# The first slice of x loaded with batch and step on the partitions and turned by TensorE, and Wx's pieces re-dealt over two DMA queues

## The chip, the cores and the metric

The kernel runs on one core of a Trainium2 chip. A core has TensorE (PE in the profile; PEld is its weight load), VectorE (DVE), ScalarE (ACT), GpSimd (POOL) and SyncE (SP); SP, ACT and POOL issue DMAs here. The metric is the device time of one execution in microseconds (us): 312.71 us is the median of three runs of the kernel before (312.63 to 312.9).

## The reference

An LSTM runs over x, and its hidden states go through a three-layer network whose weights are +1 or -1; the result is added to x.

```python
# x: (32, 64, 256)   cond: (32, 256) = first h   Wx, Wh: (256, 1024)   b: (1024,)
xW = einsum('ntd,dg->ntg', x, Wx) + b
for t in range(64):
    a = xW[:, t] + h @ Wh
    i, f, o = sigmoid(a[:, :256]), sigmoid(a[:, 256:512]), sigmoid(a[:, 512:768])
    g = tanh(a[:, 768:])
    c = f * c + i * g
    h = o * tanh(c)
    hs[:, t] = h
y = concat([hs, -hs], -1)
y = relu(s0 * y @ sign(k0)) * 2      # k0: (512, 1024) of bool
y = relu(s1 * y @ sign(k1)) * 2      # k1: (1024, 1024)
out = x + s2 * y @ sign(k2)          # k2: (1024, 256)
```

All is float32.

## The kernel before, in words

**The recurrence.** Batch N = 32, T = 64 steps, D = H = 256. The 128 partitions of the gate tiles are four column quarters q of 64 columns times 32 batch rows, so every product for a gate is four matmuls side by side, one for each quarter, with 32 output partitions each (`x_part`, L242; `gates_from_h`, L301). An x product takes as stationary operand xT, the turned x of one step (128 rows of D by 32 batch rows), and streams the columns of Wx. D is 256, so there are two parts k = 0 and 1; part k holds the rows 2p + k on partition p. A PSUM bank (`x_bank`) holds two steps. The gates lie in four slots, slot 0 the candidate g, slots 1, 2 and 3 the gates i, f, o. A float32 product is two passes on TensorE, so one product appears as two MATMUL records.

**The first eight steps.** The kernel cannot start the recurrence before the x products of the first steps exist. Before the loop TensorE does, in the order of the text (it is written out by hand, each engine executes its own part of it in that order): ten matmuls on a tile of zeros, two into the gate banks (L641) and eight more as a warm-up (L643); then the products for k = 0, slots 1 and 2, for all eight steps; k = 0, slots 0 and 3, for all eight; the bias, which is spread over the partitions by sixteen passes with a row of ones (`copy_bias`, L654) and copied by VectorE; and k = 1, all slots, step by step, where each finished bank is evicted with the bias added (`evict_x`, L258). Then come steps 8 to 11, and the loop over t, which mixes `gates_from_h` of each step with further x products (until step 21) and with the feed-forward network of finished blocks.

**The first loads.** `load_x(0, 0, ...)` fetches x of steps 0 to 7 in four DMAs of 64 KB, quarter by quarter, so that a row of 64 columns (256 bytes) is the unit; the tile has (quarter, batch) on the partitions. VectorE turns it by 32x32 blocks (`turn_x`, L226; the two calls are L644 and L645). Wx comes in six DMAs: SP carries slots 1 and 2 of k = 0, then of k = 1 (256 KB each); ACT carries slots 0 and 3 of k = 0, then of k = 1 (128 KB each). Then both queues carry x of steps 8 to 15, then Wh. GpSimd's queue carries the first h, three pieces of the bias and the three scales. A DMA gets one of eight completion semaphores in turn, so a ninth waits on its queue for the first to land, and what stands behind it on that queue waits too.

**Buffers.** x tiles rotate over four buffers, working tiles ("act") over 24, PSUM has two banks for the gates, four of the tag "pf" (x products and the warm-up's target) and two of the tag "po" (`ps_o`; the bias first).

Of the kernel before, what the change touches and what calls it, by code (L numbers as in the profile page):

```python
# [29 lines left out]
F32 = mybir.dt.float32  # L33
# [3 lines left out]
ALU = mybir.AluOpType  # L37
# [4 lines left out]
def lstm_ffn(ctx: ExitStack, tc: tile.TileContext, x, cond, wx_d, wh_d, b_d, k0_d, k1_d, k2_d, s0_d, s1_d, s2_d, out):  # L42
    nc = tc.nc
    P = 128
    N, T, D = x.shape
    H = cond.shape[1]
    G = 4 * H
    NQ = 4
    HQ = H // NQ
# [3 lines left out]
    SB = 16  # L53
    NB = T // SB
    TB = SB * N
    SH = 4
# [5 lines left out]

    FIRST_CHORE = 2
    W2_STEP = 24
    WARM_UP = 8

    SUM_STEP = 28

    const = ctx.enter_context(tc.tile_pool(name="const", bufs=1))
    wpool = ctx.enter_context(tc.tile_pool(name="wx", bufs=1))  # L70
    xpool = ctx.enter_context(tc.tile_pool(name="x", bufs=4))
# [7 lines left out]
    ps_o = ctx.enter_context(tc.tile_pool(name="ps_o", bufs=2, space=PSUM))  # L79
    ctx.enter_context(tc.manual_schedule())  # L80

    def act(shape, dtype, name):
        return apool.tile(shape, dtype, tag="act", name=name)


    xq = {}

    def load_x(i, half, engines, part=slice(0, SB // 2)):
        if part.start == 0:
            xq[i, half] = xpool.tile([P, SB // 2, HQ], F32, tag="x", name=f"x{i}_{half}")  # L90
        t0 = i * SB + half * (SB // 2)
        for q in range(NQ):
            engines[q % len(engines)].dma_start(
                out=xq[i, half][q * N : (q + 1) * N, part],
                in_=x[:, t0 + part.start : t0 + part.stop, ts(q, HQ)],
            )
# [5 lines left out]
    wx = wpool.tile([P, 2, G], F32, tag="wx", name="wx")  # L102
# [2 lines left out]
    w2 = const.tile([P, 2, FC1, P], F32R, name="w2")  # L105

    warm = const.tile([P, 40], F32, name="warm")
    nc.vector.memset(warm, 0.0)
    idle = const.tile([P, 512], mybir.dt.bfloat16, name="idle")
    nc.vector.memset(idle, 0.0)  # L110

    first = warm[:, 4 : 4 + N]
    nc.vector.memset(first[:1], 1.0)
# [4 lines left out]
    def load_gates(t, w_d, slots, engines, chunks=slice(0, 2)):  # L118

        w_rows = w_d.rearrange("(p b) g -> p b g", b=2)  # L120
        s0, n, g0 = slots[0], len(slots), GATES[slots[0]]
        if len(engines) == 1:
            halves = [slice(0, P)]
        else:
            halves = [slice(0, P // 2), slice(P // 2, P)]
        for engine, half in zip(engines, halves):
            engine.dma_start(
                out=t[half, chunks, s0 * H : (s0 + n) * H], in_=w_rows[half, chunks, g0 * H : (g0 + n) * H]
            )


    both = [nc.sync, nc.scalar]
    load_x(0, 0, both)
    for k in range(2):
        load_gates(wx, wx_d, (1, 2), [nc.sync], slice(k, k + 1))
        for slot in (0, 3):
            load_gates(wx, wx_d, (slot,), [nc.scalar], slice(k, k + 1))
    load_x(0, 1, both)
    load_gates(wh, wh_d, (1, 2), both)
    load_gates(wh, wh_d, (0,), [nc.scalar])  # L140
    load_gates(wh, wh_d, (3,), [nc.sync])

    nc.scalar.activation(warm[:, 1:2], warm[:, :1], AF.Sigmoid)
    h_first = const.tile([P, HQ], F32, name="h_first")
    nc.gpsimd.dma_start(out=h_first, in_=cond.rearrange("n (q j) -> q n j", q=NQ))
    b_rows = b_d.rearrange("(o g h) -> o g h", o=1, g=4)
    nc.gpsimd.dma_start(out=b_row[0][:1, :1], in_=b_rows[:, 3:])
    nc.gpsimd.dma_start(out=b_row[0][:1, 1:], in_=b_rows[:, :1])
    nc.gpsimd.dma_start(out=b_row[1][:1], in_=b_rows[:, 1:3])
    scales = []  # L150
    for i, s_d in enumerate((s0_d, s1_d, s2_d)):
        s = const.tile([P, 1], F32, name=f"s{i}")
# [7 lines left out]
    for i in range(2):  # L160
        t = act([P, 2, F0], U8, f"k0_{i}")
# [62 lines left out]
    xT = {}  # L224

    def turn_x(i, half, part=slice(0, SB // 2)):  # L226
        if part.start == 0:
            xT[i, half] = act([P, SB // 2, 2, N], F32, f"xT{i}_{half}")
        nc.vector.transpose(
            xT[i, half][:, part], xq[i, half][:, part].rearrange("p t (j b) -> p t b j", b=2)  # L230
        )
# [10 lines left out]
    def x_part(p, t, k, slots, start):  # L242

        i, s = divmod(t, SB // 2)
        for q in range(NQ):
            nc.tensor.matmul(  # L246
                p[q * N : (q + 1) * N, t % 2, slots],
                xT[i // 2, i % 2][:, s, k, :],
                wx_q[:, k, q, slots],
                start=start,  # L250
                stop=False,
                skip_group_check=True,
            )

    def x_bank(t):
        return ps_f.tile([P, 2, 4, HQ], F32, tag="pf", name=f"px{t}")

    def evict_x(p, t):  # L258
        xg[t] = gpool.tile([P, 2, 4 * HQ], F32, tag="xg", name=f"xg{t}")
        b = bias.rearrange("p g j -> p (g j)").unsqueeze(1).to_broadcast([P, 2, 4 * HQ])  # L260
        load[0] += 1
        nc.vector.tensor_tensor(xg[t], p.rearrange("p t g j -> p t (g j)"), b, ALU.add)  # L262
# [374 lines left out]
    outputs = deque()  # L637

    p_idle = ps_f.tile([P, TB], F32, tag="pf", name="p_idle")
    for g in gate_banks:  # L640
        nc.tensor.matmul(g, idle[:, :P], idle, start=True, stop=True)  # L641
    for n in range(WARM_UP):
        nc.tensor.matmul(p_idle, idle[:, :P], idle, start=True, stop=True)  # L643
    turn_x(0, 0, slice(0, SB // 4))  # L644
    turn_x(0, 0, slice(SB // 4, SB // 2))  # L645
    for i in range(4):
        load_bits(i)
    for half in range(2):
# [5 lines left out]
    def copy_bias():  # L654
        p_bias = ps_o.tile([P, 4, HQ], F32, tag="po", name="p_bias")
        for q in range(NQ):
            for i, t in enumerate(b_row):
                nc.tensor.matmul(  # L658
                    p_bias[q * N : (q + 1) * N, 2 * i : 2 * i + 2],
                    first,  # L660
                    t.rearrange("p g (q j) -> p q g j", q=NQ)[:, q],
                    start=(i == 0),
                    stop=True,
                    skip_group_check=True,
                )
        nc.vector.tensor_copy(bias, p_bias)

    banks = [x_bank(t) for t in range(0, SB // 2, 2)]
    for slots in (slice(1, 3), slice(0, 4, 3)):
        for t in range(SB // 2):  # L670
            x_part(banks[t // 2], t, 0, slots, t % 2 == 0 and slots.start == 1)
    copy_bias()
    for t in range(SB // 2):
        x_part(banks[t // 2], t, 1, slice(0, 4), False)
        if t % 2:
            evict_x(banks[t // 2], t - 1)
            if t == 1:
                turn_x(0, 1)
# [89 lines left out]
```

## Time and profile before

| | |
|---|---|
| median of three runs | 312.71 us (312.63 to 312.9) |
| the profiled execution's own time | 312.31 us |
| its span, first to last instruction | 310.5 us |
| outside the span | 1.8 us |
| TensorE busy | 304.5 us, 98% of the span |
| VectorE, ScalarE, GpSimd busy | 178.1, 142.0, 6.6 us |
| DMA | 10.89 MB, mean 35 GB/s; in the first 1/40 of the span 192 GB/s |

A row of a timeline gives start, duration, engine, line, operation and tiles; several like instructions in a row are merged with a count. The chain of work is followed back from the last instruction to what released it, so its pieces add up to the span. For a DMA the profile gives the time of its issue and the time from there to its landing.

### The profile page before, as it was taken

The numbers are of one execution on the slowest core, as the hardware profiler recorded it, in microseconds if no ns is written. First come the engines' busy times: TensorE is split into PE (matmuls) and PEld (weight loads), VectorE is DVE, ScalarE is ACT, GpSimd is POOL, SyncE is SP. The second block draws the span as 40 slices with busy tenths as digits, with TensorE's granted clock in tenths as the row PEclk, the third lists the DMA queues.
The fourth block names the chain that finished last, engine by engine and source line by source line (L and its number), as shares of the span: only waits on it lengthen the run. The fifth ranks groups of instructions, "written<-read, shape, count | busy, mean of one in ns | idle before, by whom it ended". The sixth has DMA issues, their size and how long they took to land.

```text
span 310.5 us, 9798 instructions
## 1 busy us (share of the span) xinstructions
PE 304.5 (98%) x4138; PEld 242.7 (78%) x4138; DVE 178.1 (57%) x530; ACT 142.0 (46%) x512; POOL 6.6 (2%) x24
## 2 busy tenths in 40 slices
PE   8999999999999999999999999999999999999994
PEld 4888888788777777777777777777777777899993
DVE  2566767777673444355754445567554434698543
ACT  0225566774564543435633434355443333886220
POOL 5300000000000000000000000000000000000000
PEclk9999999999999999999999999999999999999999
DMA  6874001142000000000010000000310000131002
GB/s 192 206 196 99 5 19 38 36 95 65 3 2 0 2 2 0 3 2 0 2 38 22 14 3 0 2 2 13 92 34 2 3 0 2 31 79 27 2 0 69
DMA packets 30587, 10.89 MB, mean 35 GB/s; under 512 B 27720, under 2 KB 29768, under 8 KB 30544
## 3 DMA queue, kind: packets, MB, share of 16 engines
q1 hardware_dynamic: 27136, 8.66, 11.2%
q10 hardware_dynamic: 3168, 1.57, 2.0%
q8 instruction: 32, 0.52, 0.7%
q0 software_dynamic: 240, 0.04, 0.1%
q14 instruction: 11, 0.09, 0.1%
HBM read 8.16 MB, written 2.10 MB: 33 GB/s over the span
## 4 chain that ended last, share of the span: by engine, by line
PE 97%; DVE 1%; ACT 0%; issue 0%; ACTq 0%
PE p L617 30%; PE gates L305 20%; PE px L246 18%; PE p L591 8%; PE po L604 7%; PE gates L452 4%; PE po L561 2%; PE r L452 2%; PE x L452 2%; PE p L479 2%; PE p_idle L643 1%; PE gates L641 0%; DVE a_7l L362 0%; DVE o L388 0%; PE p_bias L658 0%
## 5 line engine op out<-in xcount | busy, mean ns | idle before, releaser
L305 PEld LDWEIGHTS gates<-wh,hist 128*32 128x32 f32 x2016 | 54.6, 109 | 22.3 <-issue 13.4
L305 PE MATMUL gates<-wh,hist 128*32 128x192 f32 x2016 | 68.1, 275 | 0.0
L246 PE MATMUL px<-wx,xT 128*32 128x256 f32 (+1 forms) x1168 | 60.5, 353 | 0.1
L322 ACT ACTIVATE sig<-gates 128x128 f32<-128x128 f32 x64 | 17.7, 277 | 80.6 <-PE gates L305 80.4
L246 PEld LDWEIGHTS px<-wx,xT 128*32 128x32 f32 x1168 | 42.4, 110 | 11.3 <-DVE c_first L652 0.7
L326 DVE TENSOR_TENSOR kept<-sig,c 128x64 f32<-128x64 f32 x63 | 14.2, 225 | 50.0 <-ACT sig L322 49.7
L332 ACT ACTIVATE th<-c 128x64 f32<-128x64 f32 x64 | 16.4, 257 | 31.4 <-DVE c L330 31.4
L334 DVE TENSOR_TENSOR h<-sig,th 128x64 f32<-128x64 f32 x64 | 14.4, 225 | 20.7 <-ACT th L332 20.7
L262 DVE TENSOR_TENSOR xg<-px,bias 128x512 f32<-128x512 f32 x32 | 21.2, 671 | 2.8 <-PE px L246 2.3
L316 ACT COPY gates<-xg 128x192 f32<-128x192 f32 x64 | 20.0, 313 | 1.3 <-DVE xg L262 1.3
L591 PE MATMUL p<-hhi,w 128*128 128x512 f32 x48 | 19.3, 402 | 0.0
L591 PE MATMUL p<-hlo,w 128*128 128x512 f32 x48 | 19.1, 398 | 0.0
L339 DVE STREAM_TRANSPOSE hist<-h 128x64 f32<-128x64 f32 x64 | 15.7, 245 | 2.4
L330 DVE TENSOR_TENSOR c<-kept,new 128x64 f32<-128x64 f32 x64 | 14.4, 224 | 2.2
L324 ACT ACTIVATE sig<-gates 128x64 f32<-128x64 f32 x64 | 14.9, 233 | 0.1
L323 ACT ACTIVATE cand<-gates 128x64 f32<-128x64 f32 x64 | 14.0, 218 | 0.0
L328 DVE TENSOR_TENSOR new<-sig,cand 128x64 f32<-128x64 f32 x64 | 13.9, 217 | 0.0
L317 ACT COPY gates<-xg 128x64 f32<-128x64 f32 x64 | 13.0, 203 | 0.0
L591 PEld LDWEIGHTS p<-hhi,w 128*128 128x128 f32 x48 | 9.0, 188 | 2.2
L591 PEld LDWEIGHTS p<-hlo,w 128*128 128x128 f32 x48 | 9.0, 188 | 2.0
L211 ACT ACTIVATE w<-bits,nsgn,sgn 128x1024 fp32r<-128x1024 uint8 x8 | 9.9, 1241 | 0.0
L617 PE MATMUL p<-a_7h,w 128*128 128x512 f32 x24 | 9.9, 413 | 0.0
(249 smaller groups left out, 602.8 us busy)
## 6 DMA issues: line engine op xcount, KB each, us to landing
x<-in_x_dram SPq DMA_DIRECT2D x60, 64.0 KB, 2.8
out_dram<-o SPq DMA_DIRECT2D x28, 64.0 KB, 1.8
bits<-in_L_ffn_k_dram SPq DMA_DIRECT2D x10, 128.0 KB, 3.2
wx<-in_L_cond_Wx_dram SPq DMA_DIRECT2D x2, 256.0 KB, 4.2
wx<-in_L_cond_Wx_dram ACTq DMA_DIRECT2D x4, 128.0 KB, 4.6
wh<-in_L_cond_Wh_dram ACTq DMA_DIRECT2D x2, 256.0 KB, 5.6
wh<-in_L_cond_Wh_dram SPq DMA_DIRECT2D x2, 256.0 KB, 6.2
k<-in_L_ffn_k_dram SPq DMA_DIRECT2D x2, 256.0 KB, 3.1
```

The lines of the kernel that those rows point to most:

```text
L246: nc.tensor.matmul(p[q * N : (q + 1) * N, t % 2, slots], xT[i // 2, i % 2][:, s, k, :], wx_q[:, k, q, slots], start=start, stop=False, ski ...
L262: nc.vector.tensor_tensor(xg[t], p.rearrange("p t g j -> p t (g j)"), b, ALU.add)
L305: nc.tensor.matmul(g[q * N : (q + 1) * N], hT[:, k, :], wh_q[:, k, q, slots], start=False, stop=(k == 1), skip_group_check=True,)
L316: nc.scalar.copy(gates[0], x_t[:, :3])
L322: nc.scalar.activation(sig[:, 0:2, :], gates[0][:, 1:3], AF.Sigmoid)
L324: nc.scalar.activation(sig[:, 2, :], gates[1][:, 0], AF.Sigmoid)
L332: nc.scalar.activation(th, c, AF.Tanh)
L339: nc.vector.transpose(hT, h.rearrange("p (j b) -> p b j", b=2))
L452: nc.tensor.matmul(bank[pair][:, i], a(k)[:, ts(2 * pair + i, P)], b(k, n), start=first and i == 0 and k == 0 and n == 0, stop=last and k ...
L591: nc.tensor.matmul(p, w0[:, k, ts(m, P)], a[:, k, :], start=(n == 0), stop=(n == 3))
L604: nc.tensor.matmul(po[m], w2[:, m, k], a1[k][n], start=(k == 0 and n == 0), stop=(k == FC1 - 1 and n == 1))
L617: nc.tensor.matmul(p1[m], w1[:, k, ts(m, P)], a0[k][n], start=(k == 0 and n == 0), stop=(k == FC0 - 1 and n == 1),)
```

## The change

The first eight steps of x are loaded as `x_first`: (batch, step) on the partitions, batch outermost, four steps at a time, so that a row of all 256 columns (1 KB) is the unit. Steps 0 to 3 come in two DMAs of 64 KB, one on each queue, steps 4 to 7 in one of 128 KB on ACT. TensorE turns each half by two transposes against an identity (`turn_first`), and VectorE copies the two results from PSUM into the same xT tile as before, with step and batch in the order that the products want. GpSimd makes the identity (`ident`: a memset and an affine select) ahead of its DMAs.

Wx comes in six DMAs again: k = 0 slots 1 and 2 by halves of the partitions on both queues; slot 3 on SP and slot 0 on ACT, each k = 0; then k = 1, slots 1, 2 and 3 in one DMA of 384 KB on SP and slot 0 on ACT. On GpSimd's queue the bias goes ahead of the first h.

The warm-up is three matmuls before the first turn and two behind it in place of eight; the zeros tile is 128 columns, read four times over, in place of 512, and is set first. The products of k = 0 are done by halves of four steps: slots 1 and 2, then slots 0 and 3, with the second turn between the two of the first half. The bias comes behind the first two steps of k = 1 in place of ahead of them.

```diff
-    WARM_UP = 8
+    WARM_UP = (3, 2)
...
+    idle = const.tile([P, P], mybir.dt.bfloat16, name="idle")
+    nc.vector.memset(idle, 0.0)
     nc.vector.memset(warm, 0.0)
-    idle = const.tile([P, 512], mybir.dt.bfloat16, name="idle")
-    nc.vector.memset(idle, 0.0)
...
+    ident = act([P, P], F32, "ident")
+    nc.gpsimd.memset(ident, 1.0)
+    nc.gpsimd.affine_select(
+        out=ident, in_=ident, pattern=[[-1, P]], compare_op=ALU.is_equal, fill=0.0, base=0, channel_multiplier=1
+    )
...
     both = [nc.sync, nc.scalar]
-    load_x(0, 0, both)
-    for k in range(2):
-        load_gates(wx, wx_d, (1, 2), [nc.sync], slice(k, k + 1))
-        for slot in (0, 3):
-            load_gates(wx, wx_d, (slot,), [nc.scalar], slice(k, k + 1))
+    x_first = xpool.tile([P, 2, D], F32, tag="x", name="x_first")
+    for s, engine in enumerate(both):
+        engine.dma_start(out=x_first[ts(s, P // 2), 0], in_=x_in[ts(s, N // 2), :SH])
+    load_gates(wx, wx_d, (1, 2), both, slice(0, 1))
+    nc.scalar.dma_start(out=x_first[:, 1], in_=x_in[:, SH : 2 * SH])
+    load_gates(wx, wx_d, (3,), [nc.sync], slice(0, 1))
+    load_gates(wx, wx_d, (0,), [nc.scalar], slice(0, 1))
+    load_gates(wx, wx_d, (1, 2, 3), [nc.sync], slice(1, 2))
+    load_gates(wx, wx_d, (0,), [nc.scalar], slice(1, 2))
     load_x(0, 1, both)
...
-    h_first = const.tile([P, HQ], F32, name="h_first")
-    nc.gpsimd.dma_start(out=h_first, in_=cond.rearrange("n (q j) -> q n j", q=NQ))
     b_rows = b_d.rearrange("(o g h) -> o g h", o=1, g=4)
     nc.gpsimd.dma_start(out=b_row[0][:1, :1], in_=b_rows[:, 3:])
     nc.gpsimd.dma_start(out=b_row[0][:1, 1:], in_=b_rows[:, :1])
     nc.gpsimd.dma_start(out=b_row[1][:1], in_=b_rows[:, 1:3])
+    h_first = const.tile([P, HQ], F32, name="h_first")
+    nc.gpsimd.dma_start(out=h_first, in_=cond.rearrange("n (q j) -> q n j", q=NQ))
...
     p_idle = ps_f.tile([P, TB], F32, tag="pf", name="p_idle")
+    zeros = idle.unsqueeze(1).to_broadcast([P, TB // P, P])
+
+    def warm_up(n):
+        for _ in range(n):
+            nc.tensor.matmul(p_idle, idle, zeros, start=True, stop=True)
+
+    def turn_first(i):
+        p = ps_o.tile([P, 2, N, SH], F32, tag="po", name=f"px_first{i}")
+        for k in range(2):
+            nc.tensor.transpose(p[:, k].rearrange("p n t -> p (n t)"), x_first[:, i, k::2], ident)
+        for k in range(2):
+            nc.vector.tensor_copy(xT[0, 0][:, ts(i, SH), k, :], p[:, k].rearrange("p n t -> p t n"))
+
+    xT[0, 0] = act([P, SB // 2, 2, N], F32, "xT0_0")
     for g in gate_banks:
-        nc.tensor.matmul(g, idle[:, :P], idle, start=True, stop=True)
-    for n in range(WARM_UP):
-        nc.tensor.matmul(p_idle, idle[:, :P], idle, start=True, stop=True)
-    turn_x(0, 0, slice(0, SB // 4))
-    turn_x(0, 0, slice(SB // 4, SB // 2))
+        nc.tensor.matmul(g, idle, zeros, start=True, stop=True)
+    warm_up(WARM_UP[0])
+    turn_first(0)
+    warm_up(WARM_UP[1])
...
     banks = [x_bank(t) for t in range(0, SB // 2, 2)]
-    for slots in (slice(1, 3), slice(0, 4, 3)):
-        for t in range(SB // 2):
-            x_part(banks[t // 2], t, 0, slots, t % 2 == 0 and slots.start == 1)
-    copy_bias()
+    for i in range(2):
+        for slots in (slice(1, 3), slice(0, 4, 3)):
+            for t in range(i * SH, (i + 1) * SH):
+                x_part(banks[t // 2], t, 0, slots, t % 2 == 0 and slots.start == 1)
+            if i == 0 and slots.start == 1:
+                turn_first(1)
     for t in range(SB // 2):
         x_part(banks[t // 2], t, 1, slice(0, 4), False)
+        if t == 1:
+            copy_bias()
         if t % 2:
             evict_x(banks[t // 2], t - 1)
```

## The prediction

> **What bounds the kernel now.** The page first: TensorE is the chain from end to end.
>
> ```profile
> span 310.5 us, 9798 instructions
> PE 304.5 (98%) x4138; PEld 242.7 (78%) x4138; DVE 178.1 (57%) x530; ACT 142.0 (46%) x512; POOL 6.6 (2%) x24
> PE 97%; DVE 1%; ACT 0%; issue 0%; ACTq 0%
> ```
>
> TensorE runs its text in order, so a microsecond saved ahead of the loop is saved at the end, if nothing behind it has to wait for a load instead. The change touches only the head, so next comes the chain of the first 20 us (start, duration, what).
>
> ```profile
> 0.91 0.28 DVE idle L110
> ...
> 1.24 1.03 PE gates L641 x2
> 2.27 3.23 PE p_idle L643 x8
> 5.51 1.89 PE px L246 x64
> 7.39 0.12 issue
> 7.51 1.96 PE px L246 x64
> 9.47 0.47 PE p_bias L658 x16
> 9.94 6.91 PE px L246 x128
> 16.84 0.83 PE gates L305 x28
> ```
>
> The first product can't be used before 5.5; ten idle matmuls fill the time. One hole is left, at 7.39: between the two halves of part k = 0, where slots 0 and 3 are wanted. The timeline and the DMA answers for the issues in short windows say what was waited for (last column of the latter: us from issue to landing).
>
> ```profile
> 1.66 0.92 SPq L127 DMA_DIRECT2D wx<-in_L_cond_Wx_dram  x2
> 1.69 2.29 ACTq L127 DMA_DIRECT2D wx<-in_L_cond_Wx_dram  x4
> 4.32 0.77 DVE L229 STREAM_TRANSPOSE xT<-x 128x256 f32<-128x256 f32 x2 [2.02 <-DMA x<-in_x_dram]
> ...
> x<-in_x_dram ACTq DMA_DIRECT2D x1, 64.0 KB, 2.4
> x<-in_x_dram SPq DMA_DIRECT2D x1, 64.0 KB, 2.2
> ...
> wx<-in_L_cond_Wx_dram SPq DMA_DIRECT2D x1, 256.0 KB, 3.4
> wx<-in_L_cond_Wx_dram SPq DMA_DIRECT2D x1, 256.0 KB, 5.0
> wx<-in_L_cond_Wx_dram ACTq DMA_DIRECT2D x2, 128.0 KB, 5.2
> wx<-in_L_cond_Wx_dram ACTq DMA_DIRECT2D x1, 128.0 KB, 4.6
> ```
>
> x is there at 4.1 and turned at 5.1. Wx slots 1 and 2 of k = 0 land at 1.66 + 3.4 = 5.0, of k = 1 at 2.15 + 5.0 = 7.1. ACT's second piece, slot 3 of k = 0, issued at 2.19, lands at 7.4: it ends the hole. ACT's last, issued at 3.54, lands at 8.1. So this stretch has two limits: TensorE's work, and 1.25 MB (x's 256 KB, Wx's 1 MB) that take until 8.1 to land.
>
> **The change part by part.**
>
> *Earlier warm-up.* The zeros are set first and are a quarter as wide: 0.1 us (the 40-column row of L108, 0.09) in place of 0.09 + 0.27. TensorE starts at about 1.0, 0.25 earlier. Five idle matmuls at the pace of the row (3.23 / 8 = 0.40; starts 0.43 apart) end at 3.1.
>
> *x_first.* The first two pieces are 64 KB each, first in their queues, like the two whose rows show 2.2 and 2.4 from 0.73: landed at 2.9 to 3.1, when the five matmuls end. Rows of 1 KB in place of 256 bytes may help; I take nothing for it.
>
> *Identity.* GpSimd's first own instruction stands at 1.25. The memset costs between 0.1 (L756, one column) and 0.49 (VectorE, 512 columns). The affine select isn't in the trace: between 0.19 (GpSimd's one-column rows) and 0.7 (VectorE, 512 columns). Ready at 1.5 to 2.4, hidden behind x, unless GpSimd must set itself up first: it ran no arithmetic before 8.38.
>
> ```profile
> 1.25 0.88 POOL L145 DMA_DIRECT2D h_first<-in_cond_dram  x1 [0.81 <-POOLq L756]
> ...
> 3.60 1.69 POOL L153 DMA_DIRECT2D s<-in_L_ffn_s_dram  x3
> ...
> 8.38 0.24 POOL L169 TENSOR_SCALAR sgn<-s 128x1 f32<-128x1 f32 x1 [3.10 <-DMA s<-in_L_ffn_s_dram]
> ```
>
> Its last DMA issue ends at 5.29, and the 3.1 us up to 8.38 are put down to the scale's landing, so a set-up of anything up to 3.1 would be hidden there. I take zero, since the row names the DMA as the last to come, and keep 3.1 for a rival.
>
> The Trainium skill, "GPSIMD Engine Reference", section 2.1 Instruction dispatch, speaks against this part: the first call of a freshly loaded GpSimd kernel also pays about 6 us of code loading that no instruction shows. The 3.1 us above leave no room for that, if this is the same case; with 6 us the identity would come at 7.9, the products start at 9.4, and the time would be an estimated 317. No run here shows which instructions need such a load.
>
> *The transposes.* Two per turn, two passes each as for every float32 product here. A pass costs no less than 0.03 (p_bias: 0.47 / 16) and no more than an exposed 128-column weight load and a product pass in a row, 0.19 + 0.11. So a turn is 0.12 to 1.2. I take 0.7 for the first, because the idle matmuls of 512 columns start 0.43 apart there and those of L617 later 0.2 to 0.25: TensorE is at half its pace; and 0.4 for the second. First turn: 3.1 to 3.8.
>
> *Copies, and the first product.* A VectorE copy from PSUM cost 0.42 for 256 columns (L666); for 128 I take 0.3 (bounds 0.21 and 0.42). The first copy releases part k = 0 at 3.8 + 0.06 + 0.3 + 0.1 = 4.3; the copy for k = 1 is wanted much later. Two idle matmuls hold TensorE until 3.8 + 0.85 = 4.65. Slots 1 and 2 have 128 KB less ahead of them than before: at the 299 GB/s of the window from 3.1 to 3.9 (shown below) 0.45 earlier, 4.55, and no later than 5.0. So the first product stands at 4.65, against the chain's 5.51: 0.85 gained.
>
> *Then the wait that takes the hole's place.* TensorE does slots 1 and 2 of four steps (half of 1.89: 0.95), then the second turn (0.4): 6.0. Next it wants slots 0 and 3 of k = 0. Before, 1.89 us of other work was done by the time slot 3 landed, now half of it. Behind that landing stand 0.98 + 0.95 + 0.98 = 2.9 us up to the end of k = 0, which before was at 9.47. So the break-even is a landing of slot 0 at 9.47 - 2.9 = 6.55.
>
> Slot 0 is fourth on ACT's queue: 64 + 128 + 128 KB ahead of it and its own 128 make 448 KB. If SP's queue moves as many, 896 KB have moved. The ladder of landings before: 512 KB at 5.0, 1280 KB at 8.1; between them 896 KB fall on 6.55. If SP's 384 KB go whole ahead of slot 0, it is 1152 KB, 7.6; if ACT is a turn ahead, 768 KB, 6.0. I take 6.6: the middle, and a little for the 1 KB rows. End of k = 0: 9.5. Nothing gained, nothing lost.
>
> *Behind it, at zero.* k = 1 has all landed by about 8. The bias matmuls are the same sixteen; their rows of b are issued some 0.7 to 1.2 later (identity ahead, first h behind) and took 4.5 to 4.7: landed by 9, wanted past 10. The first h slips by about 2 us to 7.5; it is turned at 14.04. The scales slip by 1 us and are wanted in the loop. VectorE loses two turns (0.77) and gets four copies; it waits for TensorE there (4.8 us before L666). SP and ACT issue nine DMAs in place of ten, and x of steps 8 to 15 and Wh stand behind them as before; TensorE wants Wh at 16.8, and its last piece landed at about 14.9 (issued at 8.1, some 6.2 to 6.8 us), so 1.9 us cover it. If that cover went, the first step would wait for it.
>
> **The sum.** 0.85 earlier start, less 0.4 for the second turn, less 0.6 of wait (6.0 to 6.6), plus the old hole of 0.1: zero, or 0.1 lost, 312.4 against the profiled execution's 312.31. That execution lies 0.4 under the median of 312.71, so I say 312.8.
>
> **The rivals.**
>
> *Slot 0 lands in time* (6.0 or earlier). For it: loads that start with fewer, longer rows, and GpSimd's DMAs later. Against it, the windows of the head: with x's short rows gone the DMA still fell to half for a while (last column GB/s).
>
> ```profile
> 3.10:3.90 0.80, 0.80 (x4) 0.28 (x2) 0.00 (x0) 0.00 (x0) 0.80 (x3) 1.00 1.05 299
> 3.90:4.70 0.80, 0.80 (x4) 0.25 (x3) 0.38 (x2) 0.00 (x0) 0.80 (x2) 1.00 0.71 149
> ```
>
>  Then TensorE sets the end: 6.0 + 2.9 = 8.9, 0.55 gained, 312.15; with a landing by 5.6, a start at 4.4 and a turn of 0.25, 0.95 gained, 311.75.
>
> *Slot 0 lands last* (7.2 to 7.6), because an engine serves SP's 384 KB whole before it turns to ACT's queue. For it: SP was served first before (its slots of k = 0 at 5.0, ACT's slot 3 at 7.4). It gives 7.4 + 2.9 = 10.3, 0.8 lost, 313.5; it decides from 7.2 on.
>
> *The identity is late.* Each 0.1 by which it passes 3.1 moves the turn and the two idle matmuls behind it; it decides from 3.7 on, where the wait for slot 0 is used up (3.7 + 0.7 + 0.85 + 0.95 + 0.4 = 6.6). With the full 3.1 us and the long memset and select (5.5): turn to 6.2, idle matmuls to 7.05, then 0.95 + 0.4 + 2.9 = 11.3: 1.8 lost, 314.5. At 4.0, 313.0.
>
> *TensorE stays at half pace* into the products, because it idles or transposes where eight unbroken matmuls stood. Before, the pace had doubled by 5.5: 64 products of 128 columns took 1.89, as 128 of 256 columns took 6.91. What ends by 6.6 is free behind the wait. If it lasts through the first half of k = 0, that ends at 4.65 + 1.9 + 0.7 + 1.95 = 9.2, and k = 0 at 11.1: 1.65 lost, 314.35.
>
> On this the Trainium skill, "TensorE: Matmul & The Clock Gate", Part 4: PE-mode transpose, says that transposes don't count as busy for the clock as matmuls do. By it alone the 0.7 us of the first turn would delay full pace by about as much, most of which the wait hides; no row here shows a transpose.
>
> **How the numbers follow.** Forecast (slot 0 at 6.1 to 7.1: 312.3 to 313.3) 0.42; in time 0.24; last 0.19; late identity 0.09; half pace 0.06. The bound of 0.2%, about what a measurement of this kernel can tell from no change, is 312.09 and 313.34. Faster: most of the in-time case, 0.22. Slower: the last three but for their mild ends, and the upper edge of the forecast, 0.36. Within: 0.42. The range leaves out the best of the in-time case and the worst of the late ones: 311.8 to 314.1; the forecast's own is 312.3 to 313.3.
>
> **What would show it.** Right: the first transpose of `turn_first` near 3.1; the first x product near 4.6; the second turn near 5.6; then a hole of TensorE that ends with a landing of Wx between 6.1 and 7.1; the end of k = 0 near 9.5; no hole behind it. Wrong: an identity after 3.7, products 0.06 us apiece in place of 0.03, a wait for Wh near 16, or no hole at all.

## The result: 0.6% slower, and the profile after

The changed kernel takes 314.76 us in the median of six runs (313.63 to 315.22), the kernel before 312.84 us beside it: a ratio of 1.0063, 95% interval 1.0053 to 1.0073. That is 1.9 us lost where 0.1 was forecast. The profiled execution took 315.07 us, span 313.3 us. The changed kernel, measured once more later, took 314.08 us (313.68 to 315.87) against 312.63: 1.0058 (1.0037 to 1.0079).

The page still shows one bound, TensorE, and 2.4 us more of its busy time; the DMA now appears in the chain.

```profile
span 313.3 us, 9803 instructions
PE 306.9 (98%) x4139; PEld 242.0 (77%) x4139; DVE 178.1 (57%) x532; ACT 142.0 (45%) x512; POOL 7.1 (2%) x26
PE 96%; DMA 1%; DVE 1%; SPq 0%; issue 0%; ACT 0%; ACTq 0%
```

The chain of the first 20 us of the changed kernel (start, duration, what) answers to the one shown of before:

```profile
0.78 0.68 SPq L145
...
1.52 3.79 DMA wx<-in_L_cond_Wx_dram
5.31 0.14 issue
5.45 1.94 PE px L260 x32
7.38 0.63 PE px_first L663 x2
8.01 4.22 PE px L260 x112
12.23 0.48 PE p_bias L685 x16
12.71 6.11 PE px L260 x109
```

Two things are to be seen. The first product stands at 5.45, not at 4.65: it waits for a half of Wx's slots 1 and 2. And from there the first 32 products take 1.94 us, where 64 took 1.89 before. The bias now has 16 records of k = 1 ahead of it (16 x 0.054 = 0.86), so 12.23 here compares with 9.47 + 0.86 = 10.33 before: the end of k = 0 is 1.9 late. That is nearly all of the loss; in the profiled execution two short stalls of TensorE, about 0.25 each at 15.1 and 25.8, which no wait explains, add to it: the first step's h comes 2.2 late, the end of the span 2.8.

TensorE's timeline for the same stretch shows the pace in the durations.

```profile
1.86 1.49 PE L658 MATMUL p_idle<-idle 128*128 128x512 bf16 x3
3.56 0.67 PE L663 MATMUL px_first<-ident,x_first 128*128 128x128 f32 x2 [0.21 <-DMA x_first<-in_x_dram]
4.03 1.06 PE L658 MATMUL p_idle<-idle 128*128 128x512 bf16 x2
5.45 1.94 PE L260 MATMUL px<-wx,xT 128*32 128x128 f32 x32 [0.36 <-DMA wx<-in_L_cond_Wx_dram]
7.31 0.70 PE L663 MATMUL px_first<-ident,x_first 128*128 128x128 f32 x2
7.94 4.29 PE L260 MATMUL px<-wx,xT 128*32 128x128 f32 x112
```

The second turn takes 0.70, as long as the first; where the pace was full it took about 0.50 in the runs below. The trace's record of the granted clock begins with the rise to full pace: at 5.20 us of the span before, at 9.22 us after. (That record holds nothing ahead of the first rise, and a view of the clock prints 1.00 there; the pace of that stretch is read from durations.)

The issues and landings, from the timeline of the queues and from the DMA answers for short windows (last column of these: us from issue to landing):

```profile
0.79 0.65 ACTq L145 DMA_DIRECT2D x_first<-in_x_dram  x1
1.47 0.60 ACTq L130 DMA_DIRECT2D wx<-in_L_cond_Wx_dram  x1
1.52 1.96 SPq L130 DMA_DIRECT2D wx<-in_L_cond_Wx_dram  x3
2.75 1.09 ACTq L130 DMA_DIRECT2D wx<-in_L_cond_Wx_dram  x2
```

```profile
x_first<-in_x_dram SPq DMA_DIRECT2D x1, 64.0 KB, 2.6
wx<-in_L_cond_Wx_dram ACTq DMA_DIRECT2D x1, 128.0 KB, 3.2
wx<-in_L_cond_Wx_dram SPq DMA_DIRECT2D x1, 128.0 KB, 3.8
wx<-in_L_cond_Wx_dram ACTq DMA_DIRECT2D x1, 128.0 KB, 4.6
```

x_first was there at 3.4 on SP and 3.2 on ACT. Of the halves of slots 1 and 2, ACT's landed at 1.47 + 3.2 = 4.7 and SP's at 1.52 + 3.8 = 5.3; the first product needs both. Slot 0 of k = 0, issued on ACT at 2.75, landed at 7.3. An issue of x_first took 0.65 to 0.68 and one of a Wx half 0.60 and 0.81 (the timeline's merged rows on SP give 1.96 for three), where x's and Wx's issues took 0.44 and 0.46 before (0.88 and 0.92 for two). So the bytes start later: in the microsecond from 1.5 to 2.5 the core moved 133 GB/s before and 46 after (last column; before first).

```profile
1.50:2.50 1.00, 1.00 (x4) 0.31 (x3) 0.75 (x2) 0.00 (x0) 1.00 (x2) 1.00 0.59 133
```

```profile
1.50:2.50 1.00, 1.00 (x4) 0.40 (x3) 0.70 (x2) 0.00 (x0) 0.48 (x1) 1.00 0.22 46
```

### The profile page after: what moved, and what is told of

Read it like the earlier page. It is cut to its first block, busy times and chain, and to the rows that moved or that the text cites. A ratio compares the mean times of both kernels' runs of the same rounds, so it can differ in the third digit from the quotient of the medians.

```text
span 313.3 us, 9803 instructions
## 1 busy us (share of the span) xinstructions
PE 306.9 (98%) x4139; PEld 242.0 (77%) x4139; DVE 178.1 (57%) x532; ACT 142.0 (45%) x512; POOL 7.1 (2%) x26
## 4 chain that ended last, share of the span: by engine, by line
PE 96%; DMA 1%; DVE 1%; SPq 0%; issue 0%; ACT 0%; ACTq 0%
PE p L631 30%; PE gates L319 20%; PE px L260 18%; PE p L605 8%; PE po L618 7%; PE gates L466 4%; PE po L575 2%; PE r L466 2%; PE x L466 2%; PE p L493 2%; DMA wx<-in_L_cond_Wx_dram 1%; SPq L145 0%; DVE a_7l L376 0%; PE px_first L663 0%; DVE o L402 0%
## 5 line engine op out<-in xcount | busy, mean ns | idle before, releaser
L319 PE MATMUL gates<-wh,hist 128*32 128x192 f32 x2016 | 69.4, 275 | 0.0
L260 PE MATMUL px<-wx,xT 128*32 128x256 f32 (+1 forms) x1168 | 63.9, 360 | 0.4 <-DMA wx<-in_L_cond_Wx_dram 0.4
L340 DVE TENSOR_TENSOR kept<-sig,c 128x64 f32<-128x64 f32 x63 | 14.2, 225 | 50.5 <-ACT sig L336 50.2
```

Source lines behind the costliest of these rows:

```text
L260: nc.tensor.matmul(p[q * N : (q + 1) * N, t % 2, slots], xT[i // 2, i % 2][:, s, k, :], wx_q[:, k, q, slots], start=start, stop=False, ski ...
L319: nc.tensor.matmul(g[q * N : (q + 1) * N], hT[:, k, :], wh_q[:, k, q, slots], start=False, stop=(k == 1), skip_group_check=True,)
```

## The experiments

The theory (A): the loss has two parts. Loads that start or stand later (x_first's form, the halves of Wx, SP's 384 KB beside slot 0), worth about 0.8; and TensorE's half pace, which stays because the warm-up is broken, worth the rest. Rivals: the loads carry all of it; the turns on TensorE themselves delay the pace (C); the half pace was an accident of one profile. Each kernel ran beside the kernel before on the same chip, which took 312.48 to 312.71 us in its medians there; ratios are to it.

### The kernel before with a break in its warm-up

```diff
-    WARM_UP = 8
+    WARM_UP = 5
```

> The kernel before with five warm-up matmuls in place of eight, so that TensorE idles from about 3.4 to 5.4 us and nothing else changes. Theory A (the loss is TensorE's half pace, and that comes from a break in the busy stretch ahead of the products): the pace doubles after 8 us in place of 5.2, the first 64 products take up to 3.8 us in place of 1.9, and the time is 1.3 to 2 us over before, 314.1 to 314.9. Theory B (the loss is the later landing of Wx, the pace only follows the time since the first matmul): nothing changes, 312.6 to 313.0.

Measured 314.4 us (313.82 to 314.66), ratio 1.0054 (1.0038 to 1.007). TensorE's timeline:

```profile
2.06 2.34 PE L643 MATMUL p_idle<-idle 128*128 128x512 bf16 x5
6.17 5.10 PE L246 MATMUL px<-wx,xT 128*32 128x128 f32 x128 [1.77 <-DVE xT L229]
```

Three idle matmuls fewer, which do no work, and 128 products take 5.10 in place of 3.85; the granted clock rises at 9.09. x was also late in this profile, which lengthened the hole and moved the first product by 0.66; the pace costs the other 1.25. So a hole in front of the products costs more than a microsecond without any part of the change, and the whole loss, 1.7, is about as large as the changed kernel's.

### The changed kernel with two idle matmuls more

```diff
-    WARM_UP = (3, 2)
+    WARM_UP = (4, 3)
```

> The changed kernel with four idle matmuls ahead of the first turn and three behind it in place of three and two, so that TensorE has no hole between 1.0 and 5.4 us but the transposes. Theory A: the pace doubles by about 5.2, and nearly the whole loss of 1.9 us goes: 312.7 to 313.3. Theory C (transposes don't count as busy, so that their 0.5 us break the stretch as a hole does): the pace still doubles past 8, 314.3 to 315.2. Theory B: no gain, 314.6 or more.

Measured 314.16 us (313.2 to 316.78), ratio 1.0047 (1.0021 to 1.0072). The clock rose at 5.36, with two transposes inside the stretch before it: the turn alone doesn't hold the pace down, and C falls in that form. (That a turn counts for less than a product is not excluded; no run here separates that.) But in the profiled execution, 316.1 us, the pace was lost again. The windows (the clock is the last but two, the last GB/s):

```profile
5.40:8.70 3.30, 1.67 (x35) 1.16 (x34) 0.49 (x2) 0.00 (x0) 0.68 (x2) 1.00 1.04 294
8.80:12.10 3.30, 3.30 (x64) 3.30 (x68) 0.00 (x0) 1.49 (x2) 1.05 (x5) 0.50 0.79 207
12.30:14.30 2.00, 2.00 (x66) 1.65 (x62) 0.00 (x0) 0.00 (x0) 1.19 (x8) 1.00 1.12 251
```

At full pace TensorE ran out of products and waited, 0.27 for steps 4 to 7 of x and 1.45 for slot 0 (landed 8.66): half of the stretch idle, and the next 3.4 us at half pace. The kernel can lose either way: at half pace the products are slow, at full pace they are done early, wait for slot 0, and the pace can go. How often it went can be read from the granted clock that every run has on record, a mean over the span. One half-pace stretch of 3.413 us takes 0.0055 off it. Two of these ten runs have 0.992 and 0.993, the ones at 316.1 and 316.78 us; the other eight have 0.997 or more and lost no pace after the rise. The record holds nothing ahead of the rise, so a late rise can't be read from it.

### The kernel before with the change's order of Wx alone, and with the pieces whole

```diff
     load_x(0, 0, both)
-    for k in range(2):
-        load_gates(wx, wx_d, (1, 2), [nc.sync], slice(k, k + 1))
-        for slot in (0, 3):
-            load_gates(wx, wx_d, (slot,), [nc.scalar], slice(k, k + 1))
+    load_gates(wx, wx_d, (1, 2), both, slice(0, 1))
+    load_gates(wx, wx_d, (3,), [nc.sync], slice(0, 1))
+    load_gates(wx, wx_d, (0,), [nc.scalar], slice(0, 1))
+    load_gates(wx, wx_d, (1, 2, 3), [nc.sync], slice(1, 2))
+    load_gates(wx, wx_d, (0,), [nc.scalar], slice(1, 2))
```

> The kernel before, x and warm-up as they were, with the changed kernel's order of Wx on the two queues alone. Theory A: TensorE is busy without a break until 5.44, the pace doubles at 5.2; slots 1 and 2 of k = 0 by halves land between 4.8 and 5.6, slot 0 between 6.6 and 7.6, which is wanted at 7.4: 312.6 to 313.2. Theory B: the halves land 0.3 to 0.5 later than the whole piece did (5.0) and the products start so much later: 313.1 to 313.6.

Measured 313.88 us (313.17 to 314.87), ratio 1.004 (1.0023 to 1.0058): the order of Wx alone, without x_first and with the whole warm-up, costs 1.2 us (the medians' difference). The halves' issues took 0.54 and 0.55 here, they landed at 5.86 and 6.04, and the first product stood at 6.12; the clock rose at 7.26.

The same order with slots 1 and 2 in one DMA on SP, and slots 3 and 0 behind each other on ACT:

```diff
-    load_gates(wx, wx_d, (1, 2), both, slice(0, 1))
-    load_gates(wx, wx_d, (3,), [nc.sync], slice(0, 1))
+    load_gates(wx, wx_d, (1, 2), [nc.sync], slice(0, 1))
+    load_gates(wx, wx_d, (3,), [nc.scalar], slice(0, 1))
```

> The kernel before with the changed order of Wx but slots 1 and 2 of k = 0 whole on SP and slot 3 on ACT, so that no piece is split over halves of the partitions; the 384 KB piece of k = 1 stays. If the halves made the kernel with the new order 1.2 us slower, this is back at 312.5 to 312.9; if the 384 KB piece ahead of slot 0 did, it stays at 313.5 to 314.0, with slot 0 landing past 7.4.

Measured 313.37 us (313.0 to 313.69), ratio 1.0019 (1.0002 to 1.0035). The timeline has two holes where before has one small one:

```profile
5.57 1.95 PE L247 MATMUL px<-wx,xT 128*32 128x128 f32 x64 [0.68 <-DMA wx<-in_L_cond_Wx_dram]
8.27 1.95 PE L247 MATMUL px<-wx,xT 128*32 128x128 f32 x64 [0.75 <-DMA wx<-in_L_cond_Wx_dram]
```

The first does not count (5.57 against 5.51 before); the second is slot 0, landed at 8.13, behind the 384 KB of k = 1 that landed at 7.69. The products behind it start 0.76 later than before (8.27 against 7.51), 0.06 of it from the first product: so the 384 KB beside slot 0 cost 0.7 of TensorE's time. The run with the halves loses 0.3 to 0.5 more by the medians (0.9 lost here, 1.2 there), though the two intervals overlap, slot 3 changed its queue too, and the pace rose at 3.94 here and at 7.26 there.

### The changed kernel with the old order of Wx

```diff
-    load_gates(wx, wx_d, (1, 2), both, slice(0, 1))
     nc.scalar.dma_start(out=x_first[:, 1], in_=x_in[:, SH : 2 * SH])
-    load_gates(wx, wx_d, (3,), [nc.sync], slice(0, 1))
-    load_gates(wx, wx_d, (0,), [nc.scalar], slice(0, 1))
-    load_gates(wx, wx_d, (1, 2, 3), [nc.sync], slice(1, 2))
-    load_gates(wx, wx_d, (0,), [nc.scalar], slice(1, 2))
+    for k in range(2):
+        load_gates(wx, wx_d, (1, 2), [nc.sync], slice(k, k + 1))
+        for slot in (0, 3):
+            load_gates(wx, wx_d, (slot,), [nc.scalar], slice(k, k + 1))
```

This, like the two of the next section, has the warm-up of (4, 3).

> The changed kernel with the warm-up of four and three and with the order of Wx of before (slots 1 and 2 whole on SP, slots 0 and 3 on ACT), x of steps 4 to 7 ahead of them on ACT. Theory A: pace doubled by 5.2. Slots 1 and 2 of k = 0 land at 4.6 to 5.1, if the halves were what delayed them in the changed kernel (5.3), or at 5.3 again, if the later first packet of x was. Time 312.4 to 313.2; theory C: 314.3 or more.

Measured 313.6 us (313.57 to 314.12), ratio 1.0029 (1.0009 to 1.0049). Slots 1 and 2 landed at 6.14, with steps 4 to 7 of x now ahead of ACT's Wx; their issue took 0.80, though it is one piece over 128 partitions, as long as a half's in the same place of the changed kernel (0.81), so behind x_first a Wx issue is slow in either form. Products from 6.28 on at full pace (the clock rose at 5.75), p_bias at 11.60. x_first with its turns and this warm-up, without the new order of Wx, loses 0.9.

### x_first whole, and Wx whole

Steps 0 to 3 in one DMA of 128 partitions on SP, the rest as changed:

```diff
-    for s, engine in enumerate(both):
-        engine.dma_start(out=x_first[ts(s, P // 2), 0], in_=x_in[ts(s, N // 2), :SH])
+    nc.sync.dma_start(out=x_first[:, 0], in_=x_in[:, :SH])
```

> The changed kernel, warm-up four and three, with x of steps 0 to 3 in one DMA of 128 partitions on SP in place of two halves; the rest as changed. If the 64-partition form is what takes 0.65 us to issue and puts the first packet at 2.2 to 2.5 in place of 1.75, the issue is 0.4 to 0.5 and the first x lands by 2.8 to 3.1; if it is the row of (batch, step, 256 columns) as such, the issue stays at 0.6 or more and x lands at 3.2 or later. Time 313.2 to 314.4.

Measured 314.39 us (313.39 to 314.99), ratio 1.0055 (1.0036 to 1.0073). The issue still took 0.66 and x_first landed at 4.06. So it is not the division into halves of the partitions that makes x_first's issue slow; the form (32 batch rows, four steps, 256 columns) does, in one DMA as in two.

With Wx's slots 1 and 2 whole too, first on ACT, slot 3 behind them and slot 0 on SP (the new lines; those that they replace are left out):

```diff
+    nc.sync.dma_start(out=x_first[:, 0], in_=x_in[:, :SH])
+    load_gates(wx, wx_d, (1, 2), [nc.scalar], slice(0, 1))
+    nc.sync.dma_start(out=x_first[:, 1], in_=x_in[:, SH : 2 * SH])
+    load_gates(wx, wx_d, (3,), [nc.scalar], slice(0, 1))
+    load_gates(wx, wx_d, (0,), [nc.sync], slice(0, 1))
     load_gates(wx, wx_d, (1, 2, 3), [nc.sync], slice(1, 2))
```

> As the one before, and slots 1 and 2 of k = 0 whole and first on ACT, with x of steps 4 to 7, slot 0 and the 384 KB on SP and slot 3 on ACT: no piece is split. If splitting is the cost, slots 1 and 2 land by 4.6, the products start by 4.9, the pace doubles by 5.5, and the time is 312.2 to 312.9. If turning x on TensorE or the pace is the cost whatever the loads do, 313.2 or more.

Measured 314.42 us (313.19 to 315.23), ratio 1.0052 (1.003 to 1.0074). Slots 1 and 2, whole and first in their queue, were issued in 0.39 (a half first in the same queue took 0.59 in the run before) and landed at 3.58, but x_first only at 4.55 and slot 0 at 7.36 (third on SP). In the profiled execution, 313.34 us, the clock was up at 3.88 and p_bias stood at 11.19; the median is over a microsecond above it.

### How steady the kernel before is

> The kernel before, unchanged, for a second profile of its head. If its loads are steady from run to run, slots 1 and 2 of k = 0 land at 4.9 to 5.2 and the pace doubles at 5.1 to 5.6, as in the first profile, and the later landings of the first four experiments (5.4 to 6.1) are their edits' doing. If its loads vary by themselves, the landing is at 5.4 to 6.1 here too, and a single profile tells little on a landing.

The kernel before unchanged: 312.59 us (312.05 to 312.77), ratio 0.9991 (0.9973 to 1.001). In its profile x landed at 5.07 in place of 4.1 and Wx's slots 1 and 2 at 5.72 in place of 5.0:

```profile
2.07 3.62 PE L643 MATMUL p_idle<-idle 128*128 128x512 bf16 x8
5.85 3.80 PE L246 MATMUL px<-wx,xT 128*32 128x128 f32 x128 [0.17 <-DVE xT L229]
```

Landings that come up to a microsecond later move the first product by 0.34, and it still meets a TensorE at full pace (the clock rose at 5.80). The long unbroken warm-up doesn't only raise the pace, it hides much of the spread of the loads. Not always: of the 84 runs that the kernel before had beside the others, with medians of 312.48 to 312.71 us, five took 313.99 to 314.73 us. None of these was profiled.

### Finer pieces of x in its old form

Half of x's steps, slots 1 and 2 of k = 0, then the other half; 7 idle matmuls that begin 0.25 earlier, as in the change:

```diff
-    load_x(0, 0, both)
-    for k in range(2):
-        load_gates(wx, wx_d, (1, 2), [nc.sync], slice(k, k + 1))
-        for slot in (0, 3):
-            load_gates(wx, wx_d, (slot,), [nc.scalar], slice(k, k + 1))
+    load_x(0, 0, both, slice(0, SB // 4))
+    load_gates(wx, wx_d, (1, 2), [nc.sync], slice(0, 1))
+    load_x(0, 0, both, slice(SB // 4, SB // 2))
+    load_gates(wx, wx_d, (0,), [nc.scalar], slice(0, 1))
+    load_gates(wx, wx_d, (3,), [nc.sync], slice(0, 1))
+    load_gates(wx, wx_d, (1, 2), [nc.sync], slice(1, 2))
+    for slot in (0, 3):
+        load_gates(wx, wx_d, (slot,), [nc.scalar], slice(1, 2))
```

> The kernel before with its x in the old row form, but loaded and turned in two halves of four steps: steps 0 to 3, then Wx's slots 1 and 2 of k=0 whole on SP, then steps 4 to 7, then slot 0 of k=0 on ACT and slot 3 on SP, then the pieces of k=1; the zeros tile is set first and narrower, and there are 7 idle matmuls in place of 8. It asks whether need-ordered loads gain once neither the new x form nor the 384 KB ahead of slot 0 is in the way. Theory A (loads cost 0.8 of the change's loss through the x form and the place of slot 0, the rest is the half pace): with both away the first product comes at 4.9 to 5.3 (before 5.51) and p_bias at 8.8 to 9.3 (before 9.47) if the pace is full by 5.5: 312.0 to 312.6. If the pace stays half to 7 or later, 313 to 314. Rival (any finer order of the loads costs more in issues than it saves): first product at 5.6 or later, 312.8 to 313.5.

Measured 314.16 us (313.29 to 314.92), ratio 1.0045 (1.0029 to 1.0061): the rival's side, and beyond it. The same loads with the kernel before's own warm-up (8 matmuls, zeros as before):

> The loads of the run with two halves of four steps, with the idle matmuls exactly as before (8, zeros tile 512 wide, set second). Theory A: as steady in its pace as before, since the idle stretch ends where it did; 312.2 to 312.8, first product 5.2 to 5.5. Rival (finer loads cost more than they save): 312.8 to 313.5.

Measured 313.63 us (313.26 to 314.38), ratio 1.0033 (1.002 to 1.0045): the rival's side too. The first product stood at 5.34 (expected up to 5.3) and at 5.61 (up to 5.5), but p_bias was no earlier than before, and the larger loss came behind it. The waits of TensorE and of SP's queue (total, times, longest) in the run with 7 idle matmuls, from 2 us on:

```profile
PE px L249 <- DMA wx<-in_L_cond_Wx_dram: 2.2, 2, 1.9
```

```profile
SPq L127 <- DMA wx<-in_L_cond_Wx_dram: 1.2, 1, 1.2
SPq L127 <- DMA x<-in_x_dram: 0.6, 1, 0.6
```

Eleven DMAs of the two queues now stand ahead of k = 1 in place of seven, and from the ninth DMA of the two queues on each is issued only when an earlier one has landed. SP could issue slots 1 and 2 of k = 1 only at 5.22, when their forerunner of k = 0 had landed at 5.20, in place of 2.15; ACT the last piece at 5.41. They landed at 11.36 and 11.95, and TensorE waited 1.9 for them (0.5 with 8 idle matmuls, where they came at 10.24 and 10.73). So a finer cut of the loads costs through the number of DMAs. Part of the loss is the pace again: in both profiles the clock rose behind the first product, at 6.50 and 6.82.

### Slot 0 ahead of k = 1, and the early hole filled

From the run with everything whole, slot 0 of k = 0 moves from SP to ACT, third there:

```diff
-    load_gates(wx, wx_d, (0,), [nc.sync], slice(0, 1))
+    load_gates(wx, wx_d, (0,), [nc.scalar], slice(0, 1))
```

> The changed kernel with x_first's steps 0 to 3 whole on SP, slots 1 and 2 of k=0 whole and first on ACT, slot 3 and then slot 0 of k=0 behind them on ACT, so that the 384 KB no longer stand ahead of or beside slot 0 on its queue; warm-up (4, 3). Theory A: slot 0 lands near 6.0 (7.36 where SP carried it), the hole before its products goes, p_bias comes near 10.0 to 10.5 (11.19 there): 312.9 to 313.6 where the pace is full by 6, over 314 where it is not. Rival (the loss is not slot 0's landing but the turning and the copies themselves): p_bias stays near 11.2 although slot 0 is early, and the time stays at 314.2 to 314.6.

Measured 314.9 us in the median, but from 312.92 to 316.35: two runs of ten at 312.92 and 313.06, the others at 314.06 and above. The profile is of the fastest one; in it slot 0 landed at 5.57, the clock rose at 4.99, and the wait for slot 0 was gone:

```profile
5.70 1.01 PE px L259 x32
6.71 0.43 PE px_first L662 x2
7.14 3.64 PE px L259 x112
10.79 0.47 PE p_bias L684 x16
```

With the loads right and the pace full, x_first and the turns cost 10.79 against 10.33, and every later step is 0.46 late. The same program took 1.1 to 3.4 us more in eight of its ten runs. None of the eight was profiled, so a late rise in them is inferred; a pace lost after the rise is not the reason in seven of them, whose granted clock is 0.998 or more (the eighth has 0.995, which leaves it open). TensorE's timeline names the suspect, a hole of 0.5 behind the fourth idle matmul, where x_first (4.17) had not come yet:

```profile
1.87 1.91 PE L657 MATMUL p_idle<-idle 128*128 128x512 bf16 x4
4.31 0.67 PE L662 MATMUL px_first<-ident,x_first 128*128 128x128 f32 x2 [0.53 <-DMA x_first<-in_x_dram]
4.78 0.92 PE L657 MATMUL p_idle<-idle 128*128 128x512 bf16 x3
```

So the hole alone was filled, with two matmuls that do no work:

```diff
-    WARM_UP = (4, 3)
+    WARM_UP = (6, 3)
```

> The run before last's best loads (slots 1 and 2 whole first, slot 0 on ACT ahead of everything of k=1) with 6 idle matmuls in place of 4 ahead of the first turn, so that TensorE no longer stands idle from 3.8 to 4.3 for x_first; all else the same. That kernel ran between 312.92 and 316.35, as if by two paces. Theory A (an idle hole in the first 5.5 us is what makes the full pace come late or go again): the runs draw together, median 312.9 to 313.5, first product near 6.0, p_bias 10.6 to 11.2, granted clock up by 6 at the latest. Rival (turning on TensorE does not count as work, or the pace has nothing to do with the hole): the spread and a median of 314.5 or more stay.

Measured 313.49 us (313.03 to 314.52, ten runs), ratio 1.0016 (0.9996 to 1.0036). The median fell by 1.4 us (the kernel before stood at 312.63 and 312.71 beside the two) and the spread from 3.4 to 1.5, although the profiled chain begins its products later and ends k = 0 later than the fastest run without them:

```profile
2.08 2.56 PE p_idle L657 x6
4.63 0.44 PE px_first L662 x2
5.08 1.28 PE p_idle L657 x3
6.36 1.02 PE px L259 x32
7.37 0.43 PE px_first L662 x2
7.81 3.62 PE px L259 x112
11.43 0.47 PE p_bias L684 x16
```

No wait is left from TensorE's start on. p_bias stands at 11.43, somewhat outside what was expected (10.6 to 11.2), and the clock rose at 6.35, in place of by 6; the pace was full from the first product. Work was added in front and time won behind.

The same idle matmuls with the changed kernel's own loads:

```diff
-    WARM_UP = (3, 2)
+    WARM_UP = (6, 3)
```

> The changed kernel with its own loads and (6, 3) idle matmuls in place of (3, 2): the early holes are filled, the wait for slot 0 of k=0 (landed 7.34 and 8.34 in its two profiles) is not. Theory A in its second half (at full pace the products run out before slot 0 lands, TensorE idles there, and the pace can fall again): 313.4 to 314.6, clock up by 6 and a hole before 8.4, in some runs with a second half-pace stretch behind it. Rival (only the early holes matter): 312.9 to 313.3 and no second stretch.

Measured 314.06 us (313.65 to 314.73), ratio 1.0043 (1.0027 to 1.006), as theory A had it. The clock was up at 5.30, slot 0 landed at 7.73, TensorE waited 0.5 for it, and p_bias stood at 11.56. No second stretch of half pace is in this profile, nor, by a granted clock of 0.996 or more, in the other three runs; a stall of 0.9 at 14.2 is, for which the trace names no wait.

### The changed kernel once more

> The changed kernel once more, unchanged, on the chip of these runs: what of its first profile is its rule and what chance. Theory A: 314.2 to 315.2 in the median, Wx's slots 1 and 2 of k=0 land at 5.0 to 5.5, and the granted clock rises only after the first product (between 5.5 and 9.3). Rival (the half pace to 9.2 was one profile's accident): clock up before 5.5 and p_bias near 11.0 or earlier with the time still over 314, so that the loads alone carry the loss.

Measured 314.08 us (313.68 to 315.87). Its profiled execution, the slowest at 315.87, is not the first one repeated:

```profile
5.46 1.08 PE L260 MATMUL px<-wx,xT 128*32 128x128 f32 x32 [0.39 <-DMA wx<-in_L_cond_Wx_dram]
6.59 0.51 PE L663 MATMUL px_first<-ident,x_first 128*128 128x128 f32 x2
8.47 5.36 PE L260 MATMUL px<-wx,xT 128*32 128x128 f32 x112 [1.37 <-DMA wx<-in_L_cond_Wx_dram]
```

```profile
8.70:12.00 3.30, 3.30 (x72) 3.30 (x67) 0.00 (x0) 1.49 (x2) 1.74 (x9) 0.50 0.87 210
```

The clock rose at 5.26, earlier than expected, the first 32 products took 1.08, and slot 0 landed only at 8.34. TensorE waited 1.37 for it, and the next 3.4 us went at half pace (0.50 in the windows row). Neither theory had named this for this kernel: A expected the clock late, the rival expected it early and p_bias near 11.0; it came at 13.83. The half pace is no accident of one profile, but its place is: it comes late in one execution and is lost again in the other. Its other six runs here, and all six of the first measurement, have a granted clock of 0.996 or more, so none of them lost it again.

## Why the prediction was wrong, by its own steps

**Identity and copies: right; x_first: 0.3 late.** The memset of 128 columns took 0.20 and the affine select 0.29, ready at 1.35, so the rival of a late identity falls. x_first landed at 3.2 to 3.4 (2.9 to 3.1 forecast), a copy took 0.29 (0.3), the first turn 0.67 (0.7). That last was right by luck: a turn is two records, one for each transpose, where the prediction counted two passes for each. GpSimd's set-up was taken at zero; its select began 0.08 behind the memset. The Trainium skill, "GPSIMD Engine Reference", section 2.1, speaks of some 6 us of code loading at a first call; nothing of that was seen for these two instructions.

**"So the first product stands at 4.65": wrong by 0.8.** Slots 1 and 2 were costed by their bytes alone, at 4.55 and no later than 5.0. One half landed at 4.68, the other at 5.31 (5.27 to 5.35 in all four profiles with these loads), and the product waits for the later one. The step took nothing for the new forms: the issues of x_first and of the halves behind it took 0.60 to 0.84 each, and the first bytes moved later. Of the 0.85 to be gained 0.06 was left.

**The landing of slot 0: the rival's side.** 6.6 was taken; it was 7.34 and 8.34 in the two profiles, and 8.66 and 7.73 in the two with these loads and a longer warm-up. "Slot 0 lands last" had 7.2 to 7.6 and 0.8 lost for it, because SP's 384 KB go ahead. They did in bytes: by the packets in the trace, 381 of the 384 KB had moved when slot 0 landed at 7.34, though their own landing came at 8.02; and the run with whole pieces shows the mechanism at 0.7. An estimate, from the durations at full pace in the other runs: a full pace through the first profile of the changed kernel would have given products 5.45 to 6.46, the turn to 6.89, a wait for slot 0 to 7.48, 3.62 for 112 records, p_bias at 11.10 in place of 10.33, again 0.8. The prediction gave this rival 0.19 and kept it apart from the next; here both held together.

**TensorE at half pace: the mechanism was right and had 0.06.** It was priced at 1.65 and 314.35, near the 314.76 measured, but that is partly luck: the price had slot 0 in time and the products from 4.65 on. In the first profile the half pace took p_bias from 11.10 (estimated above) to 12.23, 1.1 beyond the wait for slot 0. What failed is that the forecast took full pace from the first product on, or by 6.6, where "what ends by 6.6 is free behind the wait": the pace doubled at 9.2, and where it doubled in time the wait for slot 0 could undo it, which the prediction didn't have at all. The five idle matmuls were costed as a filler of time, and they leave TensorE idle for 0.21 ahead of the first turn and 0.36 ahead of the first product. With nearly the same holes (0.19 and 0.39) the second profile rose at 5.26: such holes leave the rise to chance, they don't rule it out. The sign that the prediction named for this case was seen: 0.06 us apiece for the first products.

**Sum.** 0.8 for the loads and 1.1 for the pace give 1.9, the shift of k = 0 in the first profile; that the first medians differ by 1.9 too is no proof of the same shares in them. The two parts don't add up in every run: mending the loads, with the warm-up at (4, 3), left the median at 314.9, filling the early holes alone at 314.06, which is no gain on the changed kernel's second 314.08, and both together at 313.49.

What stays open: how the 1.9 us are shared over the unprofiled runs, since their granted clock shows a pace lost again but not a late rise; why a DMA of x_first's form is issued more slowly, which was seen but not taken apart; and the short holes of TensorE behind 14 us. No version here beat the kernel before.

## What to carry to other kernels

Idle matmuls in front of the first product are not only a filler: let them run unbroken until the operands are there in the worst execution, since a hole of half a microsecond there cost 1.4 us in the median of one pair of runs here; where slot 0 still came late, filling the holes gained nothing. Before ordering loads by need, count the DMAs and what each issue takes in its new form; a piece that is wanted soon must not share the engines with a large one that isn't. And look at the spread of the runs: two runs at 312.9 beside eight above 314 said more of the cause than the median did.

## What was unexpected of the hardware

TensorE's pace changes in steps of one length. In all the profiles of this study, every stretch between two changes of the granted clock, full or half, is a multiple of 3.413 us (3.413 in the two kernels that lost the pace, then 300.373; 303.786 and 307.2 in the others), and the first rise falls anywhere from 3.88 to 9.22 us of the span. The Trainium skill, "TensorE: Matmul & The Clock Gate", Part 1, describes a free-running window of 3413 ns that decides the pace; the lengths agree. Its section "Why this matters for your kernels" warns of idle gaps over about 3 us; here waits of 1.37 us (with 0.2 ahead of it) and of 1.45 us (with 0.27 ahead) inside one such stretch went with a lost pace. They give no threshold: in the run with two halves of four steps and 7 idle matmuls, whose rise at 6.50 puts a stretch from 9.92 to 13.33, a wait of 1.92 us lay in that stretch and the pace held. The two stretches that lost it also held a turn and this one did not; no run here separates the two.

An estimate from these numbers, not an experiment: if stretches end every 3.413 us, the kernel before with the change's Wx order (rise at 7.26) had an earlier chance at 3.85 and did not rise, and its sibling with whole pieces rose at 3.94, with the same instructions on TensorE up to there from 1.24 on. A tenth of a microsecond of phase between the program's start and that grid then decides over 3.3 us of half pace. That would explain why one program gives runs 2 us apart, and why a warm-up that runs on without a hole makes it less harmful. But idle time in a stretch does not sort all the cases: by the same grid the changed kernel had a chance at 5.81 and did not rise, with 0.57 idle in that stretch (0.21 and 0.36), while the kernel with slot 0 ahead rose at 4.99 with 0.53 idle and the sibling at 3.94 with 0.71 (up to 1.24). What the pace needs stays open.

Issue times differ with the form of the DMA and with what stands ahead of it. First in the queue, 256 KB of Wx over 128 partitions took 0.39, a half of it over 64 took 0.59, and x_first's first pieces, over 128 or 64, took 0.65 to 0.70. But one piece of 256 KB took 0.80 right behind x_first, and one of 128 KB over 128 partitions, elsewhere 0.33 to 0.63, took 0.82 right behind a half.
